# The factor 15 of a 4-bit layer folded into its normalizations, one rounding step on ScalarE and one VectorE step fewer

## The chip, the cores and the metric

The kernel runs on one core of one Trainium2 chip. The metric is the device time of one execution in microseconds; lower is better. A core has TensorE (PE, matrix products), VectorE (DVE), ScalarE (ACT, functions of one tensor), GpSimd (POOL) and SyncE (SP, which here starts transfers). Each works through its own instructions in a fixed order and waits for the others through semaphores.

## The reference

The input is x of 4 x 128 x 64 x 64 (images, channels, rows, columns), and four layers follow each other:

```python
# layer 0: attention over the 4096 pixels of an image
out = einsum(v, softmax(q k)); x = gamma * out + x
# layer 1: two 3x3 convolutions with 4-bit weights and 4-bit activations
qfn(x, k)       = round(x * (2**k - 1)) / (2**k - 1)
act_quant(x, k) = qfn(clip(x, 0.0, 1.0), k)
bn_eval(x)      = x * inv + (beta - mean * inv),  inv = gamma / sqrt(var + EPS)
wq1 = weight_quant(w1, 4) * mask                       # wq2 likewise
out = act_quant(bn_eval(conv3x3(x, wq1), ...1), 4)
out = bn_eval(conv3x3(out, wq2), ...2)
x   = act_quant(out + x, 4)
# layer 2: a selective scan over the 4096 pixels (256 channels, 16 states), group norm, silu
h = exp(dt * A) * h + dt * B * x;  y = sum over states of h * C
x = silu(group_norm(W_out(y * silu(z)))) + x
# layer 3: attention again
out = x + wo(softmax(k q) v)
```

With k = 4 the number of levels is 15: layer 1 clips to 0..1, multiplies by 15, rounds and divides by 15.

## The kernel before

**Order of work.** The program is written by hand-made chains of steps: Python generators such as `convolutions()`, `scans()`, `preparation()`, `energies()` (one or more for each kind of work). Ahead of each step a chain yields `op(engine, time, ...)`. The class `Order` keeps a planned clock for each engine and always emits the step that could start first, with a rank for each chain; the times in `op` are thus its costs, and what it emits is the order in which the instructions stand on each engine. A step that is marked `port=True`, and each step of GpSimd, also waits in the plan until the previous such step has ended. Changing an engine, a time or a mark in one step can therefore move other work.

**What overlaps.** The stages of attention run in the order layer 0 of images 0, 1, 2, then layer 3 of image 0, layer 0 of image 3, and layer 3 of images 1, 2, 3. Beside them run layers 1 and 2 of earlier images. Layer 2 works on 32 blocks g of 512 pixels (8 for each image), with 16 states each: 512 steps m. For each m ScalarE makes two decays `da` (L1009), VectorE multiplies (L1036), scans twice (L1044, one for each half of the channels), and, one m later, multiplies for the readout (L1026); GpSimd adds the result to y (L1061) and at the last state of a block multiplies by the gate (L1065). ScalarE also copies the last column of each scan (`hlast`, L1019).

**Layer 1.** `convolutions()` goes through each image in 8 pieces of 512 pixels. For piece k, ScalarE splits a high part off xpad (L726) and VectorE takes the low part (L728); TensorE convolves both (L704, 7 taps each); ScalarE applies the first normalization with Relu into the tile t, named q1 (L736); VectorE clips and multiplies by 15 (L739) and rounds into rpad (L741). One piece behind, the second convolution (L704, 7 taps on rpad, fp8) is normalized by ScalarE into t, named q2 (L753); VectorE adds xpad (L756), multiplies and clips below (L759), clips above and adds the constant that rounds (L761), and takes the constant off again into the fp8 tile x1 (L764). L739 and L741 are called the first chain below, L756 to L764 the second. `MAGIC` is 12582912: adding it in fp32 rounds to an integer, and subtracting it gives that integer.

The tile t has one buffer (`bufs=1`), which q1 and q2 share. All products outside the attention take turns in one PSUM bank (`bank=True`). The weights are kept as integers, so `load_layer1()` divides the scales by `unit` (15, or 15 x 15).

**Other names.** In layer 0 `energies()` makes e (L494), ScalarE takes exponentials p (L513), `products()` makes us (L556); `finish0` transposes (L643), takes a reciprocal (L636) and adds to xpad (L647). In layer 2 `preparation()` makes xh, z, dt_ps (L880) and, with L899 to L907 on VectorE, dt and ud; `output()` makes yo (L923), whose buffers are free again once the previous image's x2 is written: a square root (L242), eight Silus (L972), eight additions (L976) and eight transfers. Layer 3 uses L565 and L589 in place of L556. A fallback, `shifted()`, repeats everything in a slower form and is entered only if a sum of exponentials is out of bounds.

Of the kernel before, what the change touches and what calls it, by code (L numbers as in the profile page):

```python
# [15 lines left out]
AF = mybir.ActivationFunctionType  # L16
ALU = mybir.AluOpType
# [6 lines left out]
TB = 512  # L24
# [10 lines left out]
LEVELS = 15.0  # L35
# [4 lines left out]
MAGIC = 12582912.0  # L40
# [6 lines left out]
class Order:  # L47
# [16 lines left out]
    @staticmethod  # L64
    def op(engine, time, *needs, bank=False, table=None, port=False, lag=0.0):
        return engine, time, needs, bank, table, port or engine == "POOL", lag
# [47 lines left out]
def img(ap):  # L114
    return ap.rearrange("p (a b) -> p a b", b=W)


def inner(t, c):
    return t[:, 1 + c * ROWS : 1 + (c + 1) * ROWS, 1 : 1 + W]
# [14 lines left out]
def conv_seq_kernel(ctx: ExitStack, tc: tile.TileContext, i: dict, out: bass.AP):  # L134
    nc = tc.nc
# [24 lines left out]
    xpad = big.tile([P, WP, WP], F32, tag="xpad", name="xpad")  # L160
    rpad = big.tile([P, WP, WP], FP8, tag="rpad", name="rpad")
# [75 lines left out]
    def rsqrt(r, var):  # L237

        v = sml.tile([P, 1], F32, tag="rs_v", name="rs_v")
        t = sml.tile([P, 1], F32, tag="rs_t", name="rs_t")  # L240
        nc.vector.tensor_scalar_add(v, var, EPS)
        nc.scalar.activation(t, v, AF.Sqrt)  # L242
        nc.vector.reciprocal(r, t)
        nc.vector.tensor_mul(t, r, r)
        nc.vector.tensor_mul(t, t, v)
        nc.vector.tensor_scalar(t, t, -0.5, 1.5, ALU.mult, ALU.add)
        nc.vector.tensor_mul(r, r, t)
# [8 lines left out]
    def load_layer1():  # L256

        for k, unit in ((1, LEVELS), (2, LEVELS * LEVELS)):
            s = const.tile([P, 1], F32, tag=f"bn_s{k}", name=f"bn_s{k}")
            sh = const.tile([P, 1], F32, tag=f"bn_b{k}", name=f"bn_b{k}")  # L260
            rsqrt(s, column(f"L1_conv_var{k}"))
            nc.vector.tensor_mul(s, s, column(f"L1_conv_gamma{k}"))
            nc.vector.tensor_mul(sh, column(f"L1_conv_mean{k}"), s)
            nc.vector.tensor_sub(sh, column(f"L1_conv_beta{k}"), sh)
            nc.vector.tensor_scalar_mul(s, s, 1.0 / unit)
            bn.append((s, sh))


        for k, dt in ((1, F32R), (2, FP8)):
            w = att.tile([P, 9 * P], F32, tag="v" if k == 1 else "it", name=f"w{k}", bufs=1)  # L270
            nc.sync.dma_start(out=w, in_=i[f"L1_conv_w{k}T"])
            nc.scalar.activation(w, w, AF.Tanh)
            mx = sml.tile([P, 1], F32, tag="wmx", name="wmx")
            nc.vector.tensor_reduce(mx, w, AX.X, ALU.max, apply_absolute_value=True)
            pt = gtile("wmx_t")
            nc.tensor.transpose(pt[0:1, 0:P], mx, ident)
            m1 = sml.tile([1, 1], F32, tag="wm1", name="wm1")
            nc.vector.tensor_reduce(m1, pt[0:1, 0:P], AX.X, ALU.max)
            pb = gtile("wmx_b")
            nc.tensor.matmul(pb[:, 0:1], lhsT=ones[0:1, :], rhs=m1, start=True, stop=True)  # L280
            rec = sml.tile([P, 1], F32, tag="wrec", name="wrec")
            nc.vector.tensor_scalar_mul(rec, pb[:, 0:1], 2.0)
            nc.vector.reciprocal(rec, rec)
            nc.vector.tensor_scalar(w, w, rec, 0.5, ALU.mult, ALU.add)
            nc.vector.tensor_scalar(w, w, LEVELS, MAGIC, ALU.mult, ALU.add)
            nc.vector.tensor_scalar(w, w, MAGIC, 2.0, ALU.subtract, ALU.mult)
            wi = const.tile([P, len(TAPS), P], dt, tag=f"wint{k}", name=f"wint{k}")
            for n, (dy, dx) in enumerate(TAPS):
                t = 3 * dy + dx
                nc.vector.tensor_scalar_add(  # L290
                    wi[:, n, :], w[:, t * P : (t + 1) * P], -LEVELS, saturate=False
                )
            wint.append(wi)
# [44 lines left out]
    op, mark, release = order.op, order.mark, order.release  # L338
    x1s = []
    for k in range(2):  # L340
        t = big.tile([P, 1 + N], FP8, tag=f"x1{k}", name=f"x1{k}")
# [370 lines left out]
    def convolutions():  # L712
        for b in range(B):
            for k in range(NTB + 1):

                if k < NTB:
                    s1, b1 = bn[0]
                    need = [("xi", b, min(k + 1, NTB - 1)), ("xi", b, k)]

                    rows = xpad[:, k * ROWS : (k + 1) * ROWS + 2, :]  # L720
                    yield op("ACT", 0.8, *need)
                    xs = [
                        att.tile([P, ROWS + 2, WP], F32R, tag=f"x{t}", name=f"x{t}", bufs=1)
                        for t in "hl"
                    ]
                    nc.scalar.copy(xs[0], rows)  # L726
                    yield op("DVE", 0.86, port=True)
                    nc.vector.tensor_sub(xs[1], rows, xs[0])  # L728
                    yield op("PE", 1.65, bank=True)
                    g = gtile("conv")  # L730
                    conv(g, xs[0], wint[0], 0, range(7), stop=False)
                    yield op("PE", 1.55)
                    conv(g, xs[1], wint[0], 0, range(7), start=False)
                    yield op("ACT", 0.78)
                    t = att.tile([P, TB], F32, tag="t", name="q1", bufs=1)
                    nc.scalar.activation(t, g, AF.Relu, bias=b1, scale=s1)  # L736
                    release()
                    yield op("DVE", 0.43)
                    nc.vector.tensor_scalar(t, t, 1.0, LEVELS, ALU.min, ALU.mult)  # L739
                    yield op("DVE", 0.43)  # L740
                    nc.vector.tensor_scalar(  # L741
                        inner(rpad, k), img(t), MAGIC, MAGIC, ALU.add, ALU.subtract, saturate=False
                    )
                c = k - 1
                if c < 0:
                    continue
                s2, b2 = bn[1]
                yield op("PE", 1.75, *([("x2", b - 2, c)] if b > 1 else []), bank=True)
                g = gtile("conv")
                conv(g, rpad, wint[1], c, range(7))  # L750
                yield op("ACT", 0.78)
                t = att.tile([P, TB], F32, tag="t", name="q2", bufs=1)
                nc.scalar.activation(t, g, AF.Identity, bias=b2, scale=s2)  # L753
                release()
                yield op("DVE", 0.69, port=True)
                nc.vector.tensor_add(img(t), img(t), inner(xpad, c))  # L756
                mark("taken", b, c)
                yield op("DVE", 0.43)
                nc.vector.tensor_scalar(t, t, LEVELS, 0.0, ALU.mult, ALU.max)  # L759
                yield op("DVE", 0.43)  # L760
                nc.vector.tensor_scalar(t, t, LEVELS, MAGIC, ALU.min, ALU.add)  # L761
                yield op("DVE", 0.43)

                nc.vector.tensor_scalar_sub(  # L764
                    x1s[b % 2][:, 1 + c * TB : 1 + (c + 1) * TB], t, MAGIC, saturate=False
                )
                mark("x1", b, c)

# [341 lines left out]
def shifted(ctx, tc, i, out, ident, ones, gmat, rsqrt, bn, wint):  # L1110

    nc = tc.nc
# [14 lines left out]
    xpad = big.tile([P, WP, WP], F32, tag="xpad", name="s_xpad")  # L1127
    rpad = big.tile([P, WP, WP], FP8, tag="rpad", name="s_rpad")
# [193 lines left out]
    def layer1(x1):  # L1322
        (s1, b1), (s2, b2) = bn
        for c in range(NTB):
            g = conv(xpad, wint[0], c)
            t = att.tile([P, TB], F32, tag="r", name="q1", bufs=3)
            nc.scalar.activation(t, g, AF.Relu, bias=b1, scale=s1)
            nc.vector.tensor_scalar(t, t, 1.0, LEVELS, ALU.min, ALU.mult)
            nc.vector.tensor_scalar(
                inner(rpad, c), img(t), MAGIC, MAGIC, ALU.add, ALU.subtract, saturate=False  # L1330
            )
        for c in range(NTB):
            g = conv(rpad, wint[1], c)
            t = att.tile([P, TB], F32, tag="r", name="q2", bufs=3)
            nc.scalar.activation(t, g, AF.Identity, bias=b2, scale=s2)
            nc.vector.tensor_add(img(t), img(t), inner(xpad, c))
            nc.vector.tensor_scalar(t, t, 0.0, 1.0, ALU.max, ALU.min)
            nc.vector.tensor_scalar(t, t, LEVELS, MAGIC, ALU.mult, ALU.add)
            nc.vector.tensor_scalar(
                x1[:, c * TB : (c + 1) * TB], t, MAGIC, 1.0 / LEVELS, ALU.subtract, ALU.mult  # L1340
            )
# [226 lines left out]
```

## Time and profile before

| | |
|---|---|
| Median of 3 runs | 3625.69 us (3621.45 to 3629.59) |
| The profiled execution: its own time | 3621.05 us |
| The profiled execution: span | 3618.9 us |
| Busy: TensorE, VectorE, ScalarE, GpSimd | 3130.2, 3037.0, 2522.3, 1320.5 us |
| Mean granted TensorE clock | 0.939 of full speed |
| Piece k = 0 of image 0: start of L736 / of L756 | 156 / 200 us |
| First scan step starts / last ends | 234 / 3273 us |

Busy time is the time in which an engine had an instruction under way; waiting for a semaphore isn't in it, but waiting inside an instruction for something that no semaphore shows is. In the groups of instructions a row has the source line, the engine, the operation, what it writes and reads, the count, the busy time and the mean of one, and the idle time of the engine just ahead of it with what ended that.

### The profile page before, as it was taken

The numbers are of one execution on the slowest core, as the hardware profiler recorded it, in microseconds if no ns is written. First come the engines' busy times: TensorE is split into PE (matmuls) and PEld (weight loads), VectorE is DVE, ScalarE is ACT, GpSimd is POOL, SyncE is SP. The second block draws the span as 40 slices with busy tenths as digits, with TensorE's granted clock in tenths as the row PEclk, the third lists the DMA queues.
The fourth block names the chain that finished last, engine by engine and source line by source line (L and its number), as shares of the span: only waits on it lengthen the run. The fifth ranks groups of instructions, "written<-read, shape, count | busy, mean of one in ns | idle before, by whom it ended". The sixth has DMA issues, their size and how long they took to land.

```text
span 3618.9 us, 69982 instructions
## 1 busy us (share of the span) xinstructions
PE 3130.2 (86%) x29495; PEld 2256.7 (62%) x29495; DVE 3037.0 (84%) x2872; ACT 2522.3 (70%) x3721; POOL 1320.5 (36%) x571
## 2 busy tenths in 40 slices
PE   5999899998999998999899999989779999205999
PEld 3988688886888755555787775555435555003665
DVE  2059999999999599999999999999999999994333
ACT  3477788787778777777787777777667776534444
POOL 0014344443444134444443344444444444451000
PEclk8999999999999999999999999999889999557999
DMA  2023433343434334444333333444354444341000
GB/s 72 1 58 93 107 96 89 96 100 103 98 93 100 88 96 106 111 108 129 90 98 106 79 105 95 107 107 106 101 139 108 109 110 106 94 105 62 13 19 17
DMA packets 203652, 327.76 MB, mean 91 GB/s; under 512 B 50608, under 2 KB 53440, under 8 KB 203328
## 3 DMA queue, kind: packets, MB, share of 16 engines
q1 hardware_dynamic: 196384, 322.09, 34.2%
q8 instruction: 233, 3.82, 0.4%
q10 hardware_dynamic: 6944, 1.10, 0.2%
q14 instruction: 91, 0.75, 0.1%
HBM read 304.27 MB, written 18.87 MB: 89 GB/s over the span
## 4 chain that ended last, share of the span: by engine, by line
PE 47%; DVE 33%; ACT 9%; issue 7%; DMA 3%; ACTq 0%; POOL 0%; SPq 0%; DVEq 0%; POOLq 0%
DVE hs L1044 14%; PE us L556 13%; PE e L494 11%; PE us L565 8%; DVE hs L1036 7%; DVE hs L1026 5%; PE us L589 3%; PE conv L704 2%; ACT p L513 2%; ACT da L1009 2%; PE yo L923 2%; PE xh L793 1%; PE proj L420 1%; DMA bc<-bc_d 1%; PE proj L462 1%
## 5 line engine op out<-in xcount | busy, mean ns | idle before, releaser
L1061 POOL TENSOR_TENSOR y<-y,hs 128x1024 f32<-128x1024 f32 x512 | 1218.2, 2379 | 1913.8 <-DVE hs L1026 1856.7
L513 ACT ACTIVATE p<-e 128x1024 f32<-128x1024 f32 x1024 | 1005.4, 1018 | 320.4 <-PE e L494 298.8
L1044 DVE TENSOR_TENSOR_SCAN hs<-da,hlast,hs 128x512 f32<-128x512 f32 x896 | 1099.9, 1264 | 16.1 <-ACT da L1009 15.9
L556 PE MATMUL us<-v,p 128*128 128x129 f32 x8192 | 1016.0, 281 | 47.4 <-ACT p L513 41.0
L556 PEld LDWEIGHTS us<-v,p 128*128 128x128 f32 x8192 | 960.4, 194 | 100.1 <-ACT p L513 45.2
L1009 ACT ACTIVATE da<-dt,amat 128x512 f32<-128x512 f32 x1024 | 702.5, 691 | 289.7 <-DVE hs L1044 284.7
L1026 DVE TENSOR_TENSOR hs<-hs,bc 128x1024 f32<-128x1024 f32 x512 | 666.9, 1303 | 15.2 <-ACT hlast L1019 14.6
L1036 DVE TENSOR_TENSOR hs<-ud,bc 128x1024 f32<-128x1024 f32 x512 | 653.0, 1275 | 1.0 <-DMA bc<-bc_d 0.6
L565 PE MATMUL us<-p,v 128*32 128x256 f32 x8192 | 525.0, 387 | 39.5 <-ACT p L513 37.2
L494 PE MATMUL e<-it,v 64*128 64x256 f32 x4096 | 528.2, 398 | 18.9 <-ACT p L513 17.9
L494 PEld LDWEIGHTS e<-it,v 64*128 64x128 f32 x4096 | 382.2, 191 | 168.9 <-issue 96.3
L565 PEld LDWEIGHTS us<-p,v 128*32 128x32 f32 x8192 | 238.1, 110 | 269.4 <-issue 86.0
L589 PE MATMUL us<-p,ones 128*32 128x256 f32 x3328 | 219.8, 382 | 0.0
L494 PE MATMUL e<-it,j 64*128 64x256 f32 x2048 | 196.0, 309 | 19.0 <-ACT v L396 9.9
L494 PEld LDWEIGHTS e<-it,j 64*128 64x128 f32 x2048 | 140.7, 189 | 77.8 <-issue 28.1
L793 PEld LDWEIGHTS <-w 128*128 128x128 bf16 x576 | 53.2, 99 | 192.9 <-issue 152.5
L1019 ACT COPY hlast<-hs 128x2 f32<-128x2 f32 x448 | 85.1, 190 | 120.0 <-DVE hs L1044 115.0
L589 PEld LDWEIGHTS us<-p,ones 128*32 128x32 f32 x3328 | 102.8, 110 | 87.9 <-issue 27.0
L793 PE MATMUL z<-x,w 128*128 128x512 fp8e4 x192 | 54.7, 395 | 117.4 <-ACT sz L816 112.4
L1044 DVE TENSOR_TENSOR_SCAN hs<-da,hs 128x512 f32<-128x512 f32 x128 | 149.4, 1203 | 1.4 <-ACT da L1009 1.3
L923 PE MATMUL yo<-y,w_out 128*128 128x512 f32 x128 | 67.6, 653 | 71.8 <-POOL y L1065 66.3
L535 DVE TENSOR_TENSOR acc<-p 128x1024 f32<-128x1024 f32 x16 | 19.6, 1225 | 126.8 <-PE us L589 99.2
(166 smaller groups left out, 2693.1 us busy)
## 6 DMA issues: line engine op xcount, KB each, us to landing
bc<-bc_d SPq DMA_DIRECT2D x512, 512.0 KB, 4.8
x_in<-in_x SPq DMA_DIRECT2D x16, 512.0 KB, 7.5
xpad<-in_x SPq DMA_DIRECT2D x32, 256.0 KB, 3.2
x_d<-yo SPq DMA_DIRECT2D x32, 256.0 KB, 2.4
x_in<-x_d SPq DMA_DIRECT2D x16, 512.0 KB, 7.1
o<-x_d SPq DMA_DIRECT2D x32, 256.0 KB, 5.4
out<-o SPq DMA_DIRECT2D x32, 256.0 KB, 2.2
bc_d<-xd SPq DMA_DIRECT2D x64, 32.0 KB, 1.9
```

The source lines that it names most:

```text
L494: nc.tensor.matmul(e[k % 4 // 2][:, k % 2, k // 4, :], lhsT=jts[s][row : row + D3, col : col + P], rhs=its[s][row : row + D3, c * CB : (c ...
L513: nc.scalar.activation(p, es[t][h], AF.Exp)
L556: nc.tensor.matmul(us[:, r, 0:VP], lhsT=ps[t, h][:, k % 2, k // 4, r * P : (r + 1) * P], rhs=vts[s][:, 8 * q + k, :], start=q == 0 and k = ...
L565: nc.tensor.matmul(us[m : m + 32, 0, :], lhsT=vts[s][:, 8 * q + k, m % D3 : m % D3 + 32], rhs=ps[t, h][:, k % 2, k // 4, :], start=q == 0 ...
L589: nc.tensor.matmul(us[32 * m : 32 * m + 32, 1, :], lhsT=ones[:, 0:32], rhs=term, start=False, stop=q == NQ - 1 and k >= len(terms) - 4,)
L793: nc.tensor.matmul(g, lhsT=w3[:, k // len(rhs), lhs[k % len(rhs)] : lhs[k % len(rhs)] + P], rhs=x[:, rhs[k % len(rhs)]], start=(k == 0), s ...
L923: nc.tensor.matmul(ps, lhsT=w_out[:, h, :], rhs=y[:, h, :], start=(h == 0), stop=(h == 1))
L1009: nc.scalar.activation(da, live["in", g][0][:, h, :], AF.Exp, scale=amat[:, h, n : n + 1])
L1026: nc.vector.tensor_mul(hs, hs, bcs.pop(m)[:, 1:2, :].to_broadcast([P, 2, TB]))
L1036: nc.vector.tensor_mul(hs, ud, bcs[m][:, 0:1, :].to_broadcast([P, 2, TB]))
L1044: nc.vector.tensor_tensor_scan(hs[:, h, :], das.pop((m, h)), hs[:, h, :], hlast[:, n, h : h + 1] if g % NTB else 0.0, ALU.mult, ALU.add,)
L1061: nc.gpsimd.tensor_tensor(y, y, hss.pop(m), ALU.add)
```

## The change

The factor 15 goes into scale and shift of both normalizations, so that the tile t already holds values of 0 to 15. In the first chain one VectorE instruction clips at 15 and adds the constant, and a ScalarE copy with the bias -MAGIC writes rpad. In the second chain the addition becomes `15 * xpad + t`, one instruction clips on both sides, and one adds and takes off the constant. All VectorE steps of both chains are marked `port=True`. The fallback is changed to match.

```diff
@@ load_layer1
             nc.vector.tensor_sub(sh, column(f"L1_conv_beta{k}"), sh)
-            nc.vector.tensor_scalar_mul(s, s, 1.0 / unit)
+            nc.vector.tensor_scalar_mul(s, s, LEVELS / unit)
+            nc.vector.tensor_scalar_mul(sh, sh, LEVELS)
             bn.append((s, sh))
@@ convolutions
                     nc.scalar.activation(t, g, AF.Relu, bias=b1, scale=s1)
                     release()
-                    yield op("DVE", 0.43)
-                    nc.vector.tensor_scalar(t, t, 1.0, LEVELS, ALU.min, ALU.mult)
-                    yield op("DVE", 0.43)
-                    nc.vector.tensor_scalar(
-                        inner(rpad, k), img(t), MAGIC, MAGIC, ALU.add, ALU.subtract, saturate=False
+                    yield op("DVE", 0.43, port=True)
+                    nc.vector.tensor_scalar(t, t, LEVELS, MAGIC, ALU.min, ALU.add)
+                    yield op("ACT", 0.69)
+                    nc.scalar.activation(
+                        inner(rpad, k), img(t), AF.Copy, bias=-MAGIC, saturate=False
                     )
...
                 yield op("DVE", 0.69, port=True)
-                nc.vector.tensor_add(img(t), img(t), inner(xpad, c))
+                nc.vector.scalar_tensor_tensor(
+                    img(t), inner(xpad, c), LEVELS, img(t), ALU.mult, ALU.add
+                )
                 mark("taken", b, c)
-                yield op("DVE", 0.43)
-                nc.vector.tensor_scalar(t, t, LEVELS, 0.0, ALU.mult, ALU.max)
-                yield op("DVE", 0.43)
-                nc.vector.tensor_scalar(t, t, LEVELS, MAGIC, ALU.min, ALU.add)
-                yield op("DVE", 0.43)
-
-                nc.vector.tensor_scalar_sub(
-                    x1s[b % 2][:, 1 + c * TB : 1 + (c + 1) * TB], t, MAGIC, saturate=False
+                yield op("DVE", 0.43, port=True)
+                nc.vector.tensor_scalar(t, t, 0.0, LEVELS, ALU.max, ALU.min)
+                yield op("DVE", 0.43, port=True)
+                nc.vector.tensor_scalar(
+                    x1s[b % 2][:, 1 + c * TB : 1 + (c + 1) * TB],
+                    t,
+                    MAGIC,
+                    MAGIC,
+                    ALU.add,
+                    ALU.subtract,
+                    saturate=False,
                 )
                 mark("x1", b, c)
```

More of the change, by code (lines that the diff above doesn't have):

```diff
@@ L1327, in layer1 @@
             nc.scalar.activation(t, g, AF.Relu, bias=b1, scale=s1)
-            nc.vector.tensor_scalar(t, t, 1.0, LEVELS, ALU.min, ALU.mult)
+            nc.vector.tensor_scalar_min(t, t, LEVELS)
             nc.vector.tensor_scalar(
@@ L1335, in layer1 @@
             nc.scalar.activation(t, g, AF.Identity, bias=b2, scale=s2)
-            nc.vector.tensor_add(img(t), img(t), inner(xpad, c))
-            nc.vector.tensor_scalar(t, t, 0.0, 1.0, ALU.max, ALU.min)
-            nc.vector.tensor_scalar(t, t, LEVELS, MAGIC, ALU.mult, ALU.add)
+            nc.vector.scalar_tensor_tensor(
+                img(t), inner(xpad, c), LEVELS, img(t), ALU.mult, ALU.add
+            )
+            nc.vector.tensor_scalar(t, t, 0.0, LEVELS, ALU.max, ALU.min)
+            nc.vector.tensor_scalar_add(t, t, MAGIC)
             nc.vector.tensor_scalar(
```

## The prediction

> **What bounds the kernel now.** I read the page's busy lines and its 40 slices first, then busy times cut where the slices break, then VectorE's groups, and last single instructions of the chain that changes.
>
> ```profile
> PE 3130.2 (86%) x29495; PEld 2256.7 (62%) x29495; DVE 3037.0 (84%) x2872; ACT 2522.3 (70%) x3721; POOL 1320.5 (36%) x571
> ...
> PE   5999899998999998999899999989779999205999
> ...
> DVE  2059999999999599999999999999999999994333
> ```
>
> Over the whole span TensorE looks busier than VectorE. The slices say otherwise: TensorE falls to 2 and 0 just before the last four slices, while VectorE stands at 9 from the fourth slice to there, with one 5 in between. The stretches put numbers on it (the columns are the stretch, its length, then busy us of PE, PEld, DVE, ACT and POOL):
>
> ```profile
> 234.00:1189.00 955.00, 890.69 (x6957) 759.02 (x6956) 918.54 (x850) 754.21 (x1140) 406.84 (x170) 0.98 0.39 97
> 1189.00:1248.00 59.00, 52.47 (x380) 44.15 (x379) 19.77 (x39) 41.58 (x54) 0.37 (x1) 0.94 0.17 51
> 1248.00:3083.00 1835.00, 1660.29 (x16863) 1081.05 (x16862) 1751.73 (x1596) 1384.75 (x2089) 809.96 (x337) 0.96 0.41 107
> 3083.00:3270.00 187.00, 20.32 (x45) 7.45 (x44) 184.18 (x154) 79.77 (x127) 90.78 (x38) 0.53 0.39 99
> 3294.00:3619.00 325.00, 311.41 (x3713) 196.56 (x3713) 111.92 (x111) 144.39 (x170) 0.00 (x0) 0.97 0.07 24
> ```
>
> VectorE is 96% busy from the first scan (234) to 1189 and 95% from 1248 to 3083; then TensorE has nothing left to do (20 of 187 us) and waits for the last scans. The last image's attention, 325 us, can only start after them. So the time is: a TensorE start of 234, VectorE's scans and what is mixed into them, one gap of 59 us at 1189, and a TensorE tail. What VectorE saves between its scans should move the end one for one; what it saves in the gap or before 234 should not.
>
> The instructions concerned, by group (count | busy us, mean ns | idle before):
>
> ```profile
> L759 DVE TENSOR_SCALAR q<-q 128x512 f32<-128x512 f32 x32 | 32.0, 1001 | 1.1
> ...
> L756 DVE TENSOR_TENSOR q<-q,xpad 128x512 f32<-128x512 f32 x32 | 27.4, 858 | 14.4 <-ACT q L753 14.4
> L739 DVE TENSOR_SCALAR q<-q 128x512 f32<-128x512 f32 x32 | 26.0, 811 | 20.4 <-ACT q L736 20.3
> ...
> L741 DVE TENSOR_SCALAR rpad<-q 128x512 fp8e4<-128x512 f32 x32 | 21.9, 686 | 1.1
> ...
> L764 DVE TENSOR_SCALAR x<-q 128x512 fp8e4<-128x512 f32 x32 | 13.8, 432 | 1.1
> L761 DVE TENSOR_SCALAR q<-q 128x512 f32<-128x512 f32 x32 | 13.7, 427 | 1.1
> ```
>
> Four alike TENSOR_SCALARs have means from 427 to 1001 ns. Their medians are 426 (L739), 432 (L741), 428 (L759), and 694 for L756; the rest is a wait inside the instruction. One case in the timeline, where L756 comes right behind the readout L1026 that sets GpSimd's next addition going:
>
> ```profile
> 1285.36 1.23 DVE L1026 TENSOR_TENSOR hs<-hs,bc 128x1024 f32<-128x1024 f32 x1
> 1286.51 0.69 DVE L756 TENSOR_TENSOR q<-q,xpad 128x512 f32<-128x512 f32 x1
> 1287.23 2.47 DVE L759 TENSOR_SCALAR q<-q 128x512 f32<-128x512 f32 x1
> 1289.73 0.43 DVE L761 TENSOR_SCALAR q<-q 128x512 f32<-128x512 f32 x1
> ```
>
> L759 took 2.47 instead of 0.43 us: an addition of 2.36 us on GpSimd (median of L1061) slipped in ahead of it.
>
> **What the Trainium skill says.** "SBUF — State Buffer", section "Who interferes with whom": a VectorE instruction in its two-port mode, or with two SBUF inputs, and a GpSimd one exclude each other for the whole instruction. The waits of 2.0 us above agree. "VectorE: DVE Perf Modes", section "The perf-mode tier table (the rule you actually need)": fp32 tensor_scalar runs at twice the rate of tensor_tensor; here 427 against 694 ns. "Perfetto Trace Analysis", section "Optimizing Scalar/DVE Operations": with VectorE saturated, moving work to ScalarE can pay although it is slower there. The trace shows the saturation; the price on ScalarE is below.
>
> **The change, part by part**, each for one of 32 pieces (4 images of 8).
>
> *Removed from VectorE.* L741 (432 ns) goes to ScalarE, and one of L759 and L761 (427) vanishes; the others stay, with other constants. 859 ns x 32 = 27.5 us. The replacement of L756 by scalar_tensor_tensor is not in the trace at this shape. At 128x1024, L899 (that operation) takes 1257 and L907 (tensor_tensor) 1225 ns on average, so I price it at L756's 694, between 660 and 760 (-1 to +2 us in all). The last instruction now has two constants and writes fp8, as L741 did: 432.
>
> *Where it lies.* Counting both programs' orders by scan, and with these medians: between the first scan and the gap 16 L741 and 15 of the four-step chains stood; they save 16 x 0.432 + 15 x 0.427 = 13.3, and one L647 with its reciprocal moves behind the gap (0.9): **-14.2**. Behind the gap the old order has 12 first and 14 second chains, the new one 13 and 15, as it leaves one piece less in the gap: 12 x 0.858 + 14 x 1.981 + 12 x 0.841 + 9 x 0.914 = 56.3 against 13 x 0.426 + 15 x 1.554 + 13 x 0.841 + 10 x 0.914 = 48.9: **-7.4**. Two first chains and one second are ahead of the first scan, under TensorE: nothing, and with that cover gone -1.3.
>
> *The gap* (1189 to 1248) is set by a chain: square root, eight Silus on ScalarE, the addition L976, then on TensorE, in order, everything up to the product yo and dt_ps, then L899. From the transposes at 1198.6 to yo at 1227.4 TensorE passes six groups of us, four of e, one first convolution and two second ones. The new order has four, two, none and one. Start to start from the timeline: 2 x 1.9 + 2 x 0.66 + 3.5 + 1.63 = 10.2 us less; but two more exponentials (0.97 each) stand ahead of the Silus. **-8.3**, between -14 and +4, since ScalarE must also deliver the exponentials in time.
>
> *Waits for GpSimd.* In the old trace those above the medians sum to 12.5 (L739), 8.1 (L741), 18.4 (L759), 5.4 (L756) and 2.6 (L728): 47.0 us. By predecessor: with L1026 just ahead, L759 waited 2.0 in every case; behind two scans 3 of 13; an L739 behind L1026 waited itself in 3 of 7 (5.2 in sum); between the two scans 1.2. The new order has 10 second chains behind L1026 (20.0), 14 behind two scans (6.5), 9 first chains behind L1026 (6.7), 8 behind L1036 (0.55 each, 4.4), and between the two scans one second chain (1.2) and four L728 (1.0 each, as L739 there waited): 42.8. **-4**, between -44 (none left) and +55. The 22 waits of 2.2 us in L1026, behind GpSimd's L1065, stay.
>
> *Added to ScalarE.* A Copy of 128x512 fp32 to fp8. Nearest rows: L911 (Copy from SBUF) 715, L816 (from PSUM) 586; I take 700, so 22.4 us between 18.8 and 24. ScalarE is busy 2139 of 2790 us outside the gap between 234 and 3083 (77%), so most lies in idle time. Behind the copy queue L513 (TensorE waits for p) and L1009 (VectorE waits for da, 17.2 us in the whole run). I add **+2**; with no cover it is +22. The second convolution now waits for ScalarE. Its tile t is freed on the engine that fills it next.
>
> *Nothing:* the two set-up instructions (0.15 each, among DMA waits; 0.3 if not), the untaken fallback, table loads (105 in both orders), transfers and GpSimd's work (equal counts; the reload of xpad waits for the same first step). The first scan: one more group e stands ahead of the first second convolution (+0.7), one instruction less follows it (-0.4): 0.
>
> Sum: -14.2 - 7.4 - 8.3 - 4 + 2 = -31.9. The profiled execution took 3621.05, 4.6 under the median of the runs; from the median, 3625.7 - 32 = **3594**.
>
> **Rivals.**
> *Slower: GpSimd slips in everywhere.* If each second chain waits 2.0 between its first two steps and each first chain 1.2, it is 32 x 3.2 = 102 us against 44 for these chains: +58, less 32 with the 4 put back (28): +30, 3656. It decides above some 72 us of waits, 36 of 2.0. For: every chain behind L1026 did. Against: 31 of the 64 new chains stand behind two scans or behind L907, where waits were rare, and the chain of the first kind is now one instruction, so nothing can slip into it.
> *No change: TensorE paces the scans.* It is 93% busy before the gap, and the chain that ended last lies 47% on it. Then VectorE only waits longer: 3626. Against: 167 us of TensorE idleness at 3083.
> *Larger gain:* the order avoids 40 of the 42.8 us of waits: 3554. For: no first step stands between two scans now (7 did).
> *A worse order:* prepared chunks come later and a second gap opens, taking back what was won; it belongs to "no change" and "slower". That the copy doesn't leave VectorE is excluded by the order.
>
> **How the numbers follow.** Forecast 0.62 (3575 to 3612), larger gain 0.17, no change 0.09, slower 0.12. A measurement of this kernel tells 0.2% (7 us) from nothing. Faster 0.80, same 0.08, slower 0.12. The range, 3560 to 3634, takes in the larger gain and no change.
>
> **What would show it.** VectorE busy down by about 31 us; scalar_tensor_tensor near 0.7; its next step at 2.4 where L1026 stands ahead; the new copy at 0.6 to 0.75 on ScalarE; the gap near 50; the last scan some 32 earlier and the tail still 325. It is wrong if the last scan comes no earlier with VectorE's busy time down, or if the 2.0 us waits pass 36.

## The result, and the profile after

The changed kernel takes **3588.08 us** (median of 4 runs, 3585.6 to 3592.85) beside 3625.96 before: a ratio of **0.9898**, 95% interval 0.9881 to 0.9915, so 1.0% faster. The forecast was 3594. Its profiled execution took 3585.6 us with a span of 3583.7, which is 35.2 less than the 3618.9 of before; what follows divides these 35.2.

The page of the changed kernel, busy times and slices:

```profile
PE 3140.9 (88%) x29495; PEld 2270.8 (63%) x29495; DVE 2995.2 (84%) x2810; ACT 2535.2 (71%) x3753; POOL 1316.5 (37%) x571
...
PE   5999889998899999999889999998979989506998
...
DVE  2049999999999599999998999999989999993333
```

VectorE's busy time fell by 41.8 us (3037.0 to 2995.2) and ScalarE's rose by 12.9. The shape is the old one: one 5 in VectorE's row, then 9 (twice 8) until TensorE's 5 and 0. Cut at the new places of the first scan, the gap and the end of TensorE's work (stretch, length, busy us of PE, PEld, DVE, ACT, POOL, then clock, DMA share and GB/s):

```profile
233.00:1173.00 940.00, 860.61 (x6566) 728.96 (x6566) 899.49 (x817) 741.72 (x1131) 404.34 (x170) 0.97 0.40 99
1173.00:1227.00 54.00, 49.49 (x388) 44.05 (x387) 15.62 (x31) 40.57 (x52) 0.43 (x1) 0.97 0.16 52
1227.00:3048.00 1821.00, 1670.47 (x16786) 1104.24 (x16787) 1734.55 (x1574) 1401.01 (x2117) 810.42 (x337) 0.97 0.42 107
3048.00:3237.00 189.00, 55.29 (x504) 28.97 (x500) 185.94 (x158) 88.72 (x140) 90.64 (x39) 0.62 0.40 101
3259.00:3584.00 325.00, 311.13 (x3713) 196.72 (x3713) 111.85 (x111) 144.33 (x170) 0.00 (x0) 0.97 0.08 24
```

The scans before the gap took 940 us where they took 955, the gap 54 where it took 59, and VectorE is as full as before: 96% and 95% busy. The tail has not become shorter or longer (325). In the fourth stretch TensorE works 55 us of 189 where it worked 20 of 187, so its idle time there fell from 167 to 134 us: VectorE's last scans now end closer behind TensorE's other work.

The groups of VectorE that answer to those shown of before (count | busy us, mean ns | idle before):

```profile
L762 DVE TENSOR_SCALAR q<-q 128x512 f32<-128x512 f32 x32 | 29.9, 936 | 1.1
L757 DVE SCALAR_TENSOR_TENSOR q<-xpad,q 128x512 f32<-128x512 f32 x32 | 26.3, 822 | 14.2 <-ACT q L754 14.1
...
L764 DVE TENSOR_SCALAR x<-q 128x512 fp8e4<-128x512 f32 x32 | 15.8, 495 | 1.1
L740 DVE TENSOR_SCALAR q<-q 128x512 f32<-128x512 f32 x32 | 15.7, 492 | 16.2 <-ACT q L737 16.2
```

and the new row of ScalarE:

```profile
L742 ACT ACTIVATE rpad<-q 128x512 fp8e4<-128x512 f32 x32 | 20.1, 630 | 2.6 <-DVE q L740 2.6
```

The six rows of before sum to 134.8 us, the four of after to 87.7: 47.1 less, of which 27.5 are the two instructions and the rest is mostly waiting that went. The copy costs 630 ns, and VectorE's new sum has a median of 692, beside 694 for the addition that it replaced. (Line numbers have shifted: L736 is now L737, L753 L754, L972 L978, L1026 L1032, L1036 L1042, L1044 L1050, L1061 L1067, L976 L982. The lines shown carry the numbers of their own kernel; the text says L976 throughout for the group norm's additions.)

### The profile page after: what moved, and what is told of

Same layout as the page of the kernel before. It is cut to its first block, busy times and chain, and to the rows that moved or that the text cites. A ratio compares the mean times of both kernels' runs of the same rounds, so it can differ in the third digit from the quotient of the medians.

```text
span 3583.7 us, 69926 instructions
## 1 busy us (share of the span) xinstructions
PE 3140.9 (88%) x29495; PEld 2270.8 (63%) x29495; DVE 2995.2 (84%) x2810; ACT 2535.2 (71%) x3753; POOL 1316.5 (37%) x571
## 4 chain that ended last, share of the span: by engine, by line
PE 55%; DVE 26%; ACT 10%; issue 5%; DMA 3%; POOL 0%; ACTq 0%; SPq 0%; DVEq 0%; POOLq 0%
PE us L557 17%; PE e L495 13%; DVE hs L1050 11%; PE us L566 9%; DVE hs L1042 6%; DVE hs L1032 5%; PE us L590 3%; PE conv L705 3%; ACT da L1015 2%; ACT p L514 2%; PE xh L799 2%; PE proj L421 1%; PE yo L929 1%; PE proj L463 1%; ACT L1015 1%
## 5 line engine op out<-in xcount | busy, mean ns | idle before, releaser
L1067 POOL TENSOR_TENSOR y<-y,hs 128x1024 f32<-128x1024 f32 x512 | 1215.4, 2374 | 1890.9 <-DVE hs L1032 1837.1
L1050 DVE TENSOR_TENSOR_SCAN hs<-da,hlast,hs 128x512 f32<-128x512 f32 x896 | 1099.0, 1263 | 15.8 <-ACT da L1015 15.5
L557 PE MATMUL us<-v,p 128*128 128x129 f32 x8192 | 1030.2, 283 | 71.3 <-ACT p L514 59.9
L557 PEld LDWEIGHTS us<-v,p 128*128 128x128 f32 x8192 | 972.8, 196 | 128.5 <-ACT p L514 62.9
L1032 DVE TENSOR_TENSOR hs<-hs,bc 128x1024 f32<-128x1024 f32 x512 | 666.8, 1302 | 27.6 <-ACT hlast L1025 27.1
L1042 DVE TENSOR_TENSOR hs<-ud,bc 128x1024 f32<-128x1024 f32 x512 | 659.6, 1288 | 0.5
L495 PE MATMUL e<-it,j 64*128 64x256 f32 x2048 | 196.2, 309 | 13.8 <-ACT p L514 10.6
L495 PEld LDWEIGHTS e<-it,j 64*128 64x128 f32 x2048 | 140.6, 189 | 72.1 <-issue 22.8
L799 PEld LDWEIGHTS <-w 128*128 128x128 bf16 x576 | 53.8, 100 | 161.8 <-issue 123.2
L1050 DVE TENSOR_TENSOR_SCAN hs<-da,hs 128x512 f32<-128x512 f32 x128 | 149.0, 1202 | 5.3 <-ACT da L1015 5.2
L536 DVE TENSOR_TENSOR acc<-p,acc 128x1024 f32<-128x1024 f32 x64 | 78.4, 1225 | 56.4 <-ACT p L514 53.0
```

Of the source, the lines that this page charges most:

```text
L495: nc.tensor.matmul(e[k % 4 // 2][:, k % 2, k // 4, :], lhsT=jts[s][row : row + D3, col : col + P], rhs=its[s][row : row + D3, c * CB : (c ...
L557: nc.tensor.matmul(us[:, r, 0:VP], lhsT=ps[t, h][:, k % 2, k // 4, r * P : (r + 1) * P], rhs=vts[s][:, 8 * q + k, :], start=q == 0 and k = ...
L799: nc.tensor.matmul(g, lhsT=w3[:, k // len(rhs), lhs[k % len(rhs)] : lhs[k % len(rhs)] + P], rhs=x[:, rhs[k % len(rhs)]], start=(k == 0), s ...
L1032: nc.vector.tensor_mul(hs, hs, bcs.pop(m)[:, 1:2, :].to_broadcast([P, 2, TB]))
L1042: nc.vector.tensor_mul(hs, ud, bcs[m][:, 0:1, :].to_broadcast([P, 2, TB]))
L1050: nc.vector.tensor_tensor_scan(hs[:, h, :], das.pop((m, h)), hs[:, h, :], hlast[:, n, h : h + 1] if g % NTB else 0.0, ALU.mult, ALU.add,)
```

## The experiments

For every kernel I divide the time from the first scan step's first multiplication to the last scan's end by VectorE's instructions: **waits inside** (what an instruction took above the median of its kind), **idle** (VectorE waiting for a semaphore), and **work** (the rest). This division is called the ledger below. Ratios are to the kernel before, timed on the same chip, with 95% intervals; a difference between two kernels below is that of their ratios, times 3626. The three parts come from one profiled execution each; since a median of a few ns less, times 896 scans, already counts as some us of work, they are good to about 3 us.

| kernel | median us | ratio | stretch | work | waits inside | idle |
|---|---|---|---|---|---|---|
| before | 3625.96 | | 3038.4 | 2763.3 | 113.3 | 161.8 |
| changed | 3588.08 | 0.9898 (0.9881 to 0.9915) | 3004.4 | 2734.4 | 101.6 | 168.4 |
| new order, old work | 3617.98 | 0.9972 (0.9963 to 0.9982) | 3036.1 | 2761.9 | 115.6 | 158.6 |
| old order, new work | 3614.36 | 0.9962 (0.9948 to 0.9975) | 3034.0 | 2740.3 | 109.1 | 184.6 |
| marks only | 3645.56 | 1.0053 (1.0039 to 1.0066) | 3062.2 | 2765.6 | 85.9 | 210.7 |
| copy twice | 3592.08 | 0.9905 (0.9890 to 0.9921) | 3005.6 | 2734.4 | 103.3 | 167.9 |
| first chain only | 3595.83 | 0.9917 (0.9900 to 0.9934) | 3011.7 | 2750.0 | 109.3 | 152.4 |
| second chain only | 3641.86 | 1.0045 (1.0028 to 1.0061) | 3059.4 | 2752.5 | 98.8 | 208.1 |
| small additions | 3537.06 | 0.9752 (0.9736 to 0.9769) | 2955.5 | 2707.3 | 27.5 | 220.7 |
| Relu at the end | 3595.37 | 0.9917 (0.9901 to 0.9934) | 3003.4 | 2724.8 | 103.0 | 175.6 |
| before, output early | 3613.15 | 0.9958 (0.9945 to 0.9972) | 3030.6 | 2761.8 | 116.2 | 152.6 |
| marks only, output early | 3598.27 | 0.9918 (0.9904 to 0.9931) | 3016.8 | 2763.0 | 109.7 | 144.1 |
| changed, output early | 3597.06 | 0.9912 (0.9898 to 0.9925) | 3013.8 | 2742.5 | 105.8 | 165.5 |
| Relu, output early | 3598.85 | 0.9918 (0.9904 to 0.9931) | 3012.0 | 2724.9 | 101.7 | 185.4 |

### Work against order

The change does two things at once: it removes VectorE work, and it moves other instructions, since the steps' costs and marks changed. Two kernels cross them. In the first every other instruction stands as in the changed kernel:

```diff
                     yield op("DVE", 0.43, port=True)
-                    nc.vector.tensor_scalar(t, t, LEVELS, MAGIC, ALU.min, ALU.add)
+                    nc.vector.tensor_scalar(t, t, 1.0, LEVELS, ALU.min, ALU.mult)
+                    nc.vector.tensor_scalar(
+                        inner(rpad, k), img(t), MAGIC, MAGIC, ALU.add, ALU.subtract, saturate=False
+                    )
                     yield op("ACT", 0.69)
-                    nc.scalar.activation(
-                        inner(rpad, k), img(t), AF.Copy, bias=-MAGIC, saturate=False
-                    )
...
                 yield op("DVE", 0.43, port=True)
-                nc.vector.tensor_scalar(t, t, 0.0, LEVELS, ALU.max, ALU.min)
+                nc.vector.tensor_scalar(t, t, LEVELS, 0.0, ALU.mult, ALU.max)
+                nc.vector.tensor_scalar(t, t, LEVELS, MAGIC, ALU.min, ALU.add)
```

> The instructions of all engines in the order of the changed kernel, but with the old work inside: L741 and the fourth step of the second chain are back on VectorE (27.5 us by their medians, about 26 of them outside the gap), and no copy on ScalarE. If the removed VectorE work is what pays: 3588 + 26 = 3614, plus what the extra two-port steps wait for GpSimd, so 3612 to 3625. Rival, the new order is what pays: within 8 us of the changed kernel, 3588 to 3596.

(The sum of the second chain and its last step are the old ones too, and so are the scales.) Its ratio is 0.0074 above the changed kernel's: 27 us, as the first theory said. It is not simply 27 us of work, though: by the ledger the changed kernel has 27.5 less work and 14.0 less waits inside than this one, and 9.8 more idle time. The second kernel is the mirror image, the old steps and costs with the new instructions in them:

```diff
                     yield op("DVE", 0.43)
-                    nc.vector.tensor_scalar(
-                        inner(rpad, k), img(t), MAGIC, MAGIC, ALU.add, ALU.subtract, saturate=False
-                    )
+                    nc.scalar.activation(
+                        inner(rpad, k), img(t), AF.Copy, bias=-MAGIC, saturate=False
+                    )
```

> The old order on all engines with the new work inside: one VectorE step less in each chain, the copy on ScalarE where L741 stood. If the removed work pays: 3626 - 26 = 3600, 3595 to 3606, since the gap keeps its length. Rival, the order pays: 3618 to 3626.

It took 3614.36, neither theory's value: 14 less than before for 23.0 us less work. (The chains alone account for 25.6 less here and 26.6 less in the new order; the rest of 23.0 and 27.5 is in the medians of other lines.) The ledger shows where the rest went: idle time rose by 22.8 (its profiled execution, at the upper end of its runs, is only 4.4 shorter than that of before). Its chains, in the old places, have these groups:

```profile
L757 DVE SCALAR_TENSOR_TENSOR q<-xpad,q 128x512 f32<-128x512 f32 x32 | 30.2, 944 | 18.6 <-ACT q L754 18.6
L740 DVE TENSOR_SCALAR q<-q 128x512 f32<-128x512 f32 x32 | 29.2, 914 | 22.2 <-ACT q L737 22.2
L762 DVE TENSOR_SCALAR q<-q 128x512 f32<-128x512 f32 x32 | 27.9, 873 | 1.1
```

L740 has a mean of 914 ns here and 492 in the changed kernel: in all six places between the two scans of a step (0.8 to 1.3 us each), and in five of seven behind the readout, each after some idle time (1.3 to 2.0 us), the clip still waits for GpSimd. So the edit of the instructions is worth 27 us in the new order and 14 in the old; the new order is worth 10 with the old work and 23 with the new. Neither alone is the gain.

```diff
-                    yield op("DVE", 0.43)
+                    yield op("DVE", 0.43, port=True)     # likewise the other four
```

> The kernel before with the port marks on its five VectorE steps and no other edit: the same instructions in another order. If the work pays, this is within 8 us of 3626. Rival, the marks alone keep these steps out of GpSimd's way: most of the 44 us of waits in the chains go, 3595 to 3610.

The marks alone made it **slower**, 3645.56. They lowered the waits as the rival said (113.3 to 85.9) and still lost, because idle time rose by 48.9. The timeline of VectorE shows one place that the kernel before does not have:

```profile
1976.61 2.45 DVE L1044 TENSOR_TENSOR_SCAN hs<-da,hlast,hs 128x512 f32<-128x512 f32 x2
...
1985.62 4.22 DVE L976 SCALAR_TENSOR_TENSOR yo<-x,yo 128x512 f32<-128x512 fp8e4 x6 [0.25 <-ACT yo L972]
1998.99 0.69 DVE L756 TENSOR_TENSOR q<-q,xpad 128x512 f32<-128x512 f32 x1 [9.15 <-ACT q L753]
...
2029.27 0.43 DVE L739 TENSOR_SCALAR q<-q 128x512 f32<-128x512 f32 x1 [10.63 <-ACT q L736]
...
2038.54 1.22 DVE L1036 TENSOR_TENSOR hs<-ud,bc 128x1024 f32<-128x1024 f32 x1
```

Between 1979 and 2038 there is no scan: a second gap of 59.5 us, where the next image's group norm (L976) stands at scan step 288, with the scans of the old blocks used up.

### The two chains apart

```diff
# first chain only: load_layer1, and the changed first chain
-            nc.vector.tensor_scalar_mul(s, s, 1.0 / unit)
+            nc.vector.tensor_scalar_mul(s, s, (LEVELS if k == 1 else 1.0) / unit)
+            if k == 1:
+                nc.vector.tensor_scalar_mul(sh, sh, LEVELS)
# second chain only: the same with k == 2, and the changed second chain
# in both, the other chain keeps its old instructions, but with port=True
```

> Only the first chain is changed (15 folded into the first normalization, copy on ScalarE); the second keeps four VectorE steps, with port marks. If VectorE's work pays: 32 x 0.432 = 13.8 us less of it, 3612, 3604 to 3618. Rival, the chains pay only together or only through the order: outside that, 3620 or more.

> Only the second chain is changed (three VectorE steps); the first keeps two on VectorE, with port marks, and nothing goes to ScalarE. If VectorE's work pays: 32 x 0.427 = 13.7 us less of it, 3612, 3604 to 3618. Rival: 3620 or more.

Each removes a little over 10 us of VectorE work in the ledger (13.3 and 10.8). One is 30 us faster than before, the other 16 slower, so both expectations missed. The second-chain kernel has L976 at step 288 and a second gap (49.9 us) like the marks; the first-chain kernel has L976 at steps 155 and 284, and its first gap shrank to 14.5. With edits of this size the order can decide the sign.

### ScalarE's price

```diff
                     nc.scalar.activation(
                         inner(rpad, k), img(t), AF.Copy, bias=-MAGIC, saturate=False
                     )
+                    nc.scalar.activation(
+                        inner(rpad, k), img(t), AF.Copy, bias=-MAGIC, saturate=False
+                    )
```

> The changed kernel with the ScalarE copy into rpad issued twice, in the same order: 32 more instructions of about 0.7 us, 22 us of ScalarE. If ScalarE's idle time hides the copy, as forecast (+2 for 22 us): 3588 to 3594. Rival, ScalarE's work is on the path: 3605 to 3610.

3 us more, with intervals that overlap (0.9905 beside 0.9898): in this order another 20 us of ScalarE (the second copy's group) is nearly all hidden.

### GpSimd's price

This kernel leaves seven eighths of GpSimd's sum over the states out, so that each addition is short; the order stays.

```diff
-            nc.gpsimd.tensor_tensor(y, y, hss.pop(m), ALU.add)
+            hs = hss.pop(m)
+            nc.gpsimd.tensor_tensor(y[:, :, 0:64], y[:, :, 0:64], hs[:, :, 0:64], ALU.add)
```

> The changed kernel with GpSimd's 512 additions to y cut from 1024 to 128 elements a partition (the other seven eighths of the sum over states are left out); same order. If the waits inside VectorE's instructions are for GpSimd and lie on the path: nearly all of those above the medians go (some 30 us in the chains and L728, 46 in the readouts L1026 of the old lines, 16 in L1036), and the time falls by 60 to 95, to 3493 to 3528. Rival, TensorE is close behind VectorE and takes over: no more than 30 less, 3558 or above.

GpSimd's additions and VectorE's readouts in it:

```profile
L1068 POOL TENSOR_TENSOR y<-y,hs 128x128 f32<-128x128 f32 x512 | 238.7, 466 | 2835.5 <-DVE hs L1032 2769.8 <-DVE rall L637 21.2 <-ACT p L514 20.9
```

```profile
L1032 DVE TENSOR_TENSOR hs<-hs,bc 128x1024 f32<-128x1024 f32 x512 | 623.0, 1217 | 43.6 <-ACT hlast L1025 42.5
```

The additions fell from 2374 to 466 ns, the readout's mean from 1302 to 1217, and the waits inside from 101.6 to 27.5: most of them were waits for these additions. Of the 27.5 left, 16.9 are in the multiplication L1042, most of it in 22 instructions that start while GpSimd's multiplication by the gate runs, which kept its length (2.36 us). The ledger's 27 us less work is the multiplication too: its median fell from 1289 to 1198 ns. The time fell by 53 us, less than the 60 that was expected at least, because idle time rose by 52: about half of what VectorE is given comes back as waiting for the others.

### Is it the gap?

Over all these kernels VectorE idles 40 to 50 us around step 160 where L976 stands there (28 with the second chain only), and no more than 14 where it stands earlier; likewise 33 to 43 us from step 276 to 292 where L976 of the second image stands at 288, and no more than 18 otherwise. That made the gap look like the thing to remove. First one step less on VectorE, in the changed kernel:

```diff
-                nc.vector.tensor_scalar(t, t, 0.0, LEVELS, ALU.max, ALU.min)
-                yield op("DVE", 0.43, port=True)
-                nc.vector.tensor_scalar(x1..., t, MAGIC, MAGIC, ALU.add, ALU.subtract, saturate=False)
+                nc.vector.tensor_scalar(t, t, MAGIC, MAGIC + LEVELS, ALU.add, ALU.min)
+                yield op("ACT", 0.69)
+                nc.scalar.activation(x1..., t, AF.Relu, bias=nmagic, saturate=False)
```

> The changed kernel with one more VectorE step of the second chain gone: after the sum, one instruction adds the constant and clips above, and a Relu on ScalarE with the bias -MAGIC clips below and writes x1. 13.7 us less on VectorE, 22 more on ScalarE. If VectorE is the bound and ScalarE has idle time left: 3588 - 13 = 3575, 3565 to 3582. Rival, ScalarE's queue now delays the scans or the exponentials: 3588 or more.

It missed: 3595.37, not faster than the changed kernel (the intervals overlap) although the ledger has 9.6 us less work. The first scan came 7.7 us later (240.8 beside 233.1), and L976 of the second image stood at 288 with 33 us of idle time around it. Then four kernels in which only the rank of `output()` is changed, so that L976 stands earlier:

```diff
-            (3, output()),
+            (1, output()),
```

> The kernel before with the rank of the chain output() at 1 in place of 3: the group norm's additions L976 of the first two images now stand at scan steps 144 and 267 (160 and 281 before), ahead of the point at which the scans run out. If the gap of 59 us is there because L976 stands at step 160: it goes, VectorE's idle time falls by about 38, and the time is 3588, 3578 to 3605. Rival, the gap is TensorE's backlog and only moves: 3615 or more.

It took 3613.15, 15 less than before and not 38. The gap went from step 160 and came back at 144, where L976 now stood:

```profile
1107.04 5.11 DVE L976 SCALAR_TENSOR_TENSOR yo<-x,yo 128x512 f32<-128x512 fp8e4 x8
1130.00 0.69 DVE L756 TENSOR_TENSOR q<-q,xpad 128x512 f32<-128x512 f32 x1 [17.85 <-ACT q L753]
...
1141.39 1.22 DVE L1036 TENSOR_TENSOR hs<-ud,bc 128x1024 f32<-128x1024 f32 x1
```

34 us without a scan step, half of them waiting for L753, which takes a convolution's result over: much as the rival said, a gap that moves, though the time came out 2 us under the rival's 3615.

> The kernel with the port marks alone, which has two gaps (64 and 60 us; L976 at steps 160 and 288), with output() at rank 1: L976 at 132 and 267. If the 19 us that the marks alone lost are the second gap: both go, 3645 - 75 = 3570, 3560 to 3590, and the marks now gain or equal the same edit without them. Rival, the marks lose by themselves: some 19 slower than the kernel before with rank 1.

3598.27: 49 us less than the marks alone, where 75 were expected, and 15 less than the kernel before with the same rank. So the marks do not lose by themselves; in this order they win.

> The changed kernel with output() at rank 1: L976 at steps 134 and 259 (160 and 276 without). If the gap goes and the removed VectorE work pays as it did: 3588 - 38 = 3550, 3540 to 3565, and some 20 to 40 us under the kernel before with rank 1. Rival, without the gap TensorE is the bound and the change gains less than 10 there.

3597.06, no faster than the changed kernel (0.9912 beside 0.9898, intervals overlap) and no faster than the marks with early output (0.9918), although it has 20.5 us less VectorE work than those. Beside the kernel before with early output it is 0.0046, 17 us, faster: less than the 20 to 40 that were expected, more than the rival's 10. But the marks alone bring 15 of these 17.

> The kernel with the Relu at the end of the second chain (L976 at steps 152 and 288, a gap of 44 us at the second) with output() at rank 1: L976 at 136 and 267. If the gap at 288 and not ScalarE's load took what the removed step should bring: 3595 - 35 = 3560 or less, down to 10 us under the changed kernel with rank 1, 3535 to 3562. Rival, ScalarE's load costs as much as VectorE saves: at or above the changed kernel with rank 1.

3598.85: another 17.6 us less work, and again nothing. In these three kernels the work falls from 2763.0 to 2742.5 to 2724.9 while idle time rises from 144.1 to 165.5 to 185.4, and the stretch stays at 3012 to 3017. VectorE's work is **not** the bound there. But two things change with it: the order is a little different each time, and each step taken from VectorE puts 20 to 23 us on ScalarE. VectorE's idle time by the engine whose result ended it says where the gain went:

| kernel | idle, ended by ScalarE | by TensorE |
|---|---|---|
| marks only, output early | 86.7 | 48.0 |
| changed, output early | 110.7 | 47.6 |
| Relu, output early | 132.3 | 46.6 |

The waits for the decays `da` are the line that grew most:

```profile
DVE hs L1044 <- ACT da L1009: 12.4, 9, 3.9
...
DVE hs L1050 <- ACT da L1015: 31.5, 15, 5.8
```

The first line is of the marks with early output, the second of the Relu with early output (us in total, times, the longest). So what VectorE saved came back as waiting for ScalarE, as the last run's rival said. Whether ScalarE was late because of its added steps, because of the order, or because it waited for TensorE itself, no run separates.

No kernel with the whole computation in it beats the changed one.

## Why the prediction was right

The forecast, 32 us less, was measured as 38 between the medians and 35.2 between the profiled executions. By its own steps:

- **Removed work.** The ledger has 28.9 us less, some 3 of it because the scans' median is 6.5 ns shorter in this profile. Before the gap it is 15.6 less (forecast -14.2), behind it 8.8 less (-7.4). The stretch behind the gap is shorter by 13.8 (2024.4 to 2010.6), since its waits inside fell too (70.6 to 62.2) and its idle time rose only from 86.1 to 89.5.
- **The gap**, forecast -8.3, gave -5.3 (58.9 to 53.6). The part from the transposes to yo came out as worked: 28.8 us before, 17.1 now (1190.46 to 1207.61 on TensorE); behind yo it is 1.4 less. The mis-sized term is what stands ahead of it: from the last scan to the transposes 17.2 us in place of 9.4, +7.8 where the two extra exponentials were to cost 1.9. Of these, 5.2 are the square root that opens the chain. VectorE hands over its input at 1173.3, but on ScalarE two exponentials, which wait 1.78 us for TensorE, and the table load stand ahead of it; before, the table load had ended 1.4 us before the input came, and VectorE waited 0.27:

```profile
1175.31 1.94 ACT L514 ACTIVATE p<-e 128x1024 f32<-128x1024 f32 x2 [1.78 <-PE e L495]
1177.26 1.28 ACT L242 ACT_TABLE_LOAD   x1
1178.56 0.20 ACT L242 ACTIVATE rs_t<-rs_v 128x1 f32<-128x1 f32 x1
...
1178.79 0.17 DVE L243 RECIPROCAL grs<-rs_t 128x1 f32<-128x1 f32 x1 [5.45 <-ACT rs_t L242]
```

TensorE in the gap of the changed kernel, from the transposes to yo:

```profile
1190.46 0.60 PE L644 MATMUL ut<-ident,us 128*128 128x128 f32 x4
...
1200.88 1.69 PE L705 MATMUL conv<-rpad,wint 128*128 128x512 fp8e4 x7
...
1207.61 1.99 PE L929 MATMUL yo<-y,w_out 128*128 128x512 f32 x4
```

- **Waits for GpSimd** were the term most under-sized: 42.8 us were forecast for the chains and L728 together, 29.8 were measured beside 47.0 before, so -17 and not -4. The ten second chains behind the readout waited as forecast, each about 2 us. This is the worst of them, in the timeline of the changed kernel:

```profile
794.26 1.21 DVE L1032 TENSOR_TENSOR hs<-hs,bc 128x1024 f32<-128x1024 f32 x1
795.40 0.68 DVE L757 SCALAR_TENSOR_TENSOR q<-xpad,q 128x512 f32<-128x512 f32 x1
796.11 2.46 DVE L762 TENSOR_SCALAR q<-q 128x512 f32<-128x512 f32 x1
798.61 2.47 DVE L764 TENSOR_SCALAR x<-q 128x512 fp8e4<-128x512 f32 x1
```

The rest hardly waited: none of the 14 behind two scans more than 0.2 us (6.5 forecast), none behind the multiplication, which the forecast called L1036 (4.4), none between scans (5.2), and one of nine first chains behind the readout (1.6 us, 6.7 forecast). Before, four of seven of these waited in their second step, L741, and in the changed kernel there is none on VectorE. Two L728 behind a readout waited 2.1 us each, which the forecast did not have. Part came back in that multiplication, whose waits grew by 6.7 us (9.2 to 15.9); the new order with the old work has the same (16.3), so this is of the order.
- **ScalarE** (+2): the copy is 630 ns, not 700; doubling it cost about 3 us. All idle time rose by 6.6, outside the gap by 7.4; how much of that is the copy's is not shown, but with the copy doubled it stayed (168.4 and 167.9).
- **First scan and tail** (0): -1.0 and -0.1.

Put together, the profiled executions differ by -24.4 (work outside the gap), -5.3 (gap), -11.8 (waits outside the gap), +7.4 (idle time outside the gap) and -1.1 (start and tail): -35.2. The forecast had -21.6, -8.3, -4, +2 and 0. So the work was sized well, and the total came as near as it did partly by luck: the waits fell by more than was forecast, the gap by less, and idle time rose by more. (Two slips in it do not bear on the sum: the larger gain, 3554, lies outside the range 3560 to 3634 that is said to take it in, and the alike TENSOR_SCALARs shown are five, not four.)

What does not hold as a rule is the sentence that carries the sum, that what VectorE saves between its scans moves the end one for one. In the order that the change happens to make, the edit brought 27 us for 27.5 of work, but as a sum of work, waits and idle time, as the crossed runs show. In the old order 23.0 us of work gave 14, and in three orders with early output 38 us of work, with 43 us more on ScalarE, gave nothing. The rival "TensorE paces the scans" was rated at 0.09; it did not hold for the change. The runs with early output do not show it either: VectorE's waits for TensorE stayed at 47 to 48 us there. But the 167 us of TensorE idleness cited against it say only that TensorE finishes early, not that it is on time for each step. The rival "a worse order" was real too: the marks alone and the second chain alone made a second gap and were slower. The changed kernel's second-image L976 stood at step 276, ahead of 288, where those two kernels had it; the order told this beforehand and the prediction did not use it.

What stays open: what sets the 3012 to 3017 us of the early orders. The idle time that grew was ended by ScalarE, but it is spread over a dozen lines, none above 32 us; no run in these orders changed ScalarE's work alone, and none took work from TensorE.

## What to carry to other kernels

When an order is planned by costs, an edit is two edits: the work it removes and the order it makes. Run them crossed, old work in the new order and new work in the old, before crediting either. Work taken from a 96% busy engine need not shorten the time one for one: here much the same work taken out brought 27, 14 or next to nothing. See where its idle time stands and which engine ends it, since a shorter instruction may come back as a longer wait.

## What was not expected of the hardware

A wait for GpSimd inside a VectorE instruction depends on what stands just ahead: in the changed kernel, behind the readout that starts an addition, ten of ten second chains waited 1.4 to 2.0 us in one of their first two steps, and behind two scans none of 14 waited more than 0.2 (3 of 13 waited 2.0 in the kernel before). Shortening the additions to 466 ns took away 74 of 102 us of waits inside, shortened the multiplication's median from 1289 to 1198 ns and brought 53 us of time. A Copy with an immediate bias from SBUF to fp8 on ScalarE took 630 ns, where the Copy of 128x512 with a column as its scale, written as fp32, takes 714 in the same kernel.
